# A scan kernel with its exponentials in another memory: `da` moved from PSUM to SBUF, banks and buffers shared out anew

## The chip, the cores and the metric

The kernel runs on one core of a Trainium2 chip. The metric is the time of one execution on the device, in microseconds. An engine is called by its short name in the profile: PE multiplies matrices, DVE is the vector engine, ACT the scalar engine, POOL the engine that the code calls `gpsimd`, SP the one whose queue issues the DMAs (`sync`). SBUF is the working memory; PSUM has eight banks of 128 x 512 fp32 values, into which PE writes.

## What is computed

The input is `x`, 8 images of 384 channels and 32 x 32 points, all in fp32. Layer 0 is a hybrid: a state-space recurrence in both directions along the 1024 points, plus a gated 3 x 3 convolution. Layer 1 is causal attention and a feed-forward network over the 1024 tokens. Cut to what matters here:

```python
# layer 0, for each direction
u = silu(conv1d(xn @ in_w)); z = xn @ in_w2
dt, Bm, Cm = split(u @ x_proj_w)
delta = softplus(dt @ dt_proj_w + dt_proj_b)
deltaA  = exp(delta[..., None] * A)                    # 16 states per channel
deltaBu = (delta * u)[..., None] * Bm[:, :, None, :]
h = dA * h + dBu                                       # along the 1024 points
y = (sum over states of h * C + u * D_param) * silu(z)
x = x + res_scale * ((fwd + bwd) @ out_w * scale_mod + sigmoid(conv2d(xn)) * xn)
# layer 1
t = t + attention(layernorm(t))                        # causal, one head
t = t + gelu(layernorm(t) @ kron(c_fc_1, c_fc_2).T) @ kron(c_proj_1, c_proj_2).T
```

## The kernel before, in words

**The recurrence.** A state of a channel takes a partition: 32 channels times 4 states fill the 128 partitions, and 512 points lie along the free axis. Each image (`b`) is worked off in four steps, `STEPS`: two directions times two halves of 512 points. A step has 12 units (3 groups of 128 channels `cc` times 4 groups of states `g`), so the kernel has 8 x 4 x 12 = 384 units. A unit (in `scan`) does the following:

- DMAs spread `delta` to four tiles `dl`, `delta * u` to one tile `du` of 128 x 2048 (a buffer of tag `hs`), and the rows of B and C to `br` and `cr`.
- POOL makes `hs = du * br` in one product of 128 x 2048.
- ACT makes four exponentials `da` of 128 x 512, at line 1054 in a buffer of the PSUM pool `ps_b` (5 banks).
- DVE runs four `tensor_tensor_scan` over `da` and `hs`. In a "split" unit the scan writes over `da`, and DVE then multiplies `da` by `cr` into `hs`. In the other units (`POOL_C`, 4 of 12; `POOL_END`, 5 of 12, in the last image) the scan writes into `hs` and POOL multiplies all of `hs` by `cr`.
- ACT copies the last column of a scan to `carry`, for the step that continues it.
- PE sums over the states by four matmuls `y <- hs, sel` into the PSUM bank `y`. D u comes in through one matmul with the diagonal matrix `ddiag`.

The last step of the last image is cut into two parts of 256 points.

**The rest.** `norm_in`, `raw_gate`, `conv_tokens`, `prepare`, `conv`, `local` and `gate` prepare the next image; `project` multiplies y by the output weights and adds the local branch and x; `attention` and `feed_forward` are layer 1, on halves of 512 tokens. All of it runs in between the units of the recurrence. PSUM is shared out as five banks for `da`, two for this side work (tag `w`, handed out by `bank`), one for `y`; in the last image's end `rota` lets the side work use `da` banks too. Transit tiles come in two pools, `tmp` (5) and `side` (4). The four large weights `win`, `wz`, `wout`, `wvs` are loaded once and stay. `prepare` sums u of two steps on POOL, so that D u enters once for both directions; `local` adds x on POOL.

**The order.** The program's instructions are recorded with a due time (`plan.due`, in units) and a margin (`plan.rush`). `Plan.order` then plays a model of the engines and issues, engine by engine, the most urgent instruction whose inputs and buffers would be there. It also places filler matmuls (`y <- zero, ident`) where PE would pause. So the constants at the head (`FIRST`, `OTHERS`, `LAYER1`, `SCAN` and others) are due times. Each engine executes its own queue in the order that this gave. In the profile nearly all instructions have line 460, the one in `issue` that calls them; they are told apart by their tiles.

Of the kernel before, what the change touches and what calls it, by code (L numbers as in the profile page):

```python
# [30 lines left out]
P = 128  # L31
# [4 lines left out]
TMP, SIDE = 5, 4  # L36
REPS = 4
RUSH = 3.54
START, LATER = -40.0, -8.0
# [3 lines left out]
FIRST = (1.62, 3.96, 10.3, 14.48, 18.18, 21.76)  # L43
SECOND = (22.86, 0.54)
OTHERS = (4.13, 9.04, 14.9, 17.86, 22.66, 25.08, 29.09, 34.25, 42.87, 49.8)
BURST = 8.07
PROJECT = 1.35
LAYER1 = (39.85, 51.29, 60.87, 72.21, 83.5)
LAYER1_6 = (43.34, 50.01, 57.44, 69.38, 72.99)
LAYER1_7 = (39.84, 42.87, 51.35, 57.52, 62.56, 71.14, 71.63, 74.06, 81.9)  # L50
HASTE = 26.32
FREE = ["w", "da", "w", "da"]
EXPS = -0.17
SCAN = (-1.49, -1.1, -0.44, -0.43, -0.36, 0.14, 0.08, 1.19, 0.79)
DU_AHEAD = 3.37
DL_AHEAD = 3.22
DLS = 5
DAS = 5
# [22 lines left out]
class Plan:  # L81
# [9 lines left out]
    LOOSE = ("w", "tmp", "side")  # L91
    HURRY = 8.29
    PATIENCE = 1.77
    TAIL = dict(tensor=0.21, vector=0.117, scalar=0.14, gpsimd=0.1, sync=0.1)
    RAW = 0.07
    NEXT = 0.01
    TURN = 0.1
# [203 lines left out]
    def order(self):  # L301
# [73 lines left out]
        while issued < total:  # L375
            best = None
            for e in engines:
                ts = [(at(op), op) for op in cand[e]]
                ts = [(t, op) for t, op in ts if t is not None]
                if not ts:  # L380
                    continue
                now = max(clock[e], min(t for t, _ in ts))
                if best is None or now < best[0]:
                    best = (now, e, ts)
# [3 lines left out]
            op = min((op for t, op in ts if t <= now), key=lambda op: op.rank)  # L388
# [14 lines left out]
            if e == "tensor" and self.nothing and now > clock[e]:  # L403

                y = [name for name in left_y if name in self.slot and users[name]]
                begun = bool(y) and left_y[y[0]] not in (0, all_y[y[0]])
                if begun or not y and max([last[n] for n in left_y if n in last], default=0.0) < clock[e]:
                    made = self._fill(max(array) + self.TURN * (form != (P, P)), now, begun)
                    started += made
                    if made:  # L410
                        array = [self.ran[-1][1]] * 4
                        form = P, P
                        now = max(now, array[0] + self.TURN * (op.form != form))
# [50 lines left out]
def conv_attn_kernel(  # L464
# [44 lines left out]
    ps_b = ctx.enter_context(tc.tile_pool(name="ps_b", bufs=1, space=bass.MemoryType.PSUM))  # L509
# [3 lines left out]
    rota = ["w"]  # L513

    def bank():
        rota.append(rota.pop(0))
        if rota[-1] == "w":
            return plan.tile(ps_w, [P, HB], "w", 8 - 1 - DAS)
        return plan.tile(ps_b, [P, HB], "da", DAS)
# [31 lines left out]
    win = load(in_wT[:, :C].rearrange("(cc p) e -> p cc e", p=P), [P, NC, C], "win")  # L551
# [25 lines left out]
    taps, flat = (plan.tile(l0, [P, HB], "side", SIDE)[: C // BC, :P] for _ in range(2))  # L577
# [21 lines left out]
    none = plan.tile(l0, [P, HB], "side", SIDE)[:, : NC * (WP + 1)]  # L599
# [13 lines left out]
    whose = plan.tile(l0, [P, HB], "side", SIDE)[:CG, :P]  # L613
# [23 lines left out]
    for cc in range(NC):  # L637
# [17 lines left out]
        plan.tile(l0, [P, HB], "side", SIDE)[: C // BC, : KW * KW * BC] for _ in range(2)  # L655
# [21 lines left out]
    wz = load(in_wT[:, C:].rearrange("(cc p) e -> p cc e", p=P), [P, NC, C], "wz")  # L677
    wout = load(out_wT.rearrange("(cc p) e -> p cc e", p=P), [P, NC, C], "wout")
    wvs = load(wv.rearrange("(cc p) e -> p cc e", p=P), [P, NC, C], "wvs")

    fc1s = weight([P, NF, P], "fc1s")
    for to in range(NG):
        for g in range(NG):
            plan.sync.dma_start(
                fc1s[to * NJ : (to + 1) * NJ, g::NG], fc1[g * NJ : (g + 1) * NJ]
            )
    fc1f = fc1s.rearrange("p f e -> p (f e)")
    plan.gpsimd.tensor_scalar_mul(fc1f, fc1f, 1.0 / NG)
# [20 lines left out]
    every = weight([P, NJ], "every")  # L709
    plan.vector.tensor_add(every, ident[:, :NJ], ident[:, NJ : 2 * NJ])  # L710
    for g in range(2, NG):
        plan.vector.tensor_add(every, every, ident[:, g * NJ : (g + 1) * NJ])
    emat = weight([P, NJ, NI], "emat")
    plan.vector.tensor_mul(
        emat,
        every.unsqueeze(2).to_broadcast([P, NJ, NI]),
        cp2.unsqueeze(1).to_broadcast([P, NJ, NI]),
    )
    emat = emat.rearrange("p j i -> p (j i)")
    plan.tile(ps_y, [P, HB], "y")  # L720
# [18 lines left out]
    def norm_in(b, h):  # L739
        xt = load_x(b, h)  # L740
        yield
# [36 lines left out]
    def raw_gate(b, h):  # L778

        xn, z = xn_t[b, h], plan.tile(dram, [P, NC, HB], "zr", 4)  # L780
# [51 lines left out]
    def local(b, h):  # L832

        cols = slice(h * HB, (h + 1) * HB)
# [4 lines left out]
        for cc in range(NC):  # L839
            xt = tmp()  # L840
            plan.sync.dma_start(xt, xv[b, :, cc, cols])
# [5 lines left out]
            plan.gpsimd.tensor_add(xt, xt, sg[:, cc])  # L847
            plan.sync.dma_start(lx[cc * P : (cc + 1) * P], xt)
# [55 lines left out]
    def prepare(b, steps):  # L904
# [45 lines left out]
        ud = ud_t[b, steps[0]] = plan.tile(dram, [C, HB], "ud", 4)  # L950
        for cc in range(NC):
            u = uc_t[b, steps[0]][:, cc]
            for si in steps[1:]:
                both = tmp()
                plan.gpsimd.tensor_add(both, u, uc_t[b, si][:, cc])
                u = both
            plan.sync.dma_start(ud[cc * P : (cc + 1) * P], u)
# [13 lines left out]
    def side():  # L971
        return plan.tile(l0, [P, HB], "side", SIDE)

    def scan(b, si, lo=0, hi=HB):
# [5 lines left out]
        ud = ud_t.get((b, si))  # L980
# [25 lines left out]
        for k in range(n_u):  # L1006
            cc, g = divmod(k, SG)
            t = t0 + f * k
            if g == 0:
# [19 lines left out]
                parts = []  # L1029
                if ud is not None:  # L1030
                    parts.append((ddiag[:, cc], ud[cc * P : (cc + 1) * P, lo:hi]))
# [6 lines left out]
                y = plan.tile(ps_y, [P, HB], "y")[:, :n]  # L1038
# [12 lines left out]
            for i in range(NQ):  # L1051
                j = cc * NQ + i
                plan.due, plan.rush = t + f * SCAN[1 + i], EXPS
                da = plan.tile(ps_b, [P, HB], "da", DAS)[:, :n]
# [7 lines left out]
                if split:  # L1062
                    if save:
                        plan.due, plan.rush = t + f * SCAN[5] * (i + 0.1), RUSH
                        plan.scalar.copy(carry[:, k, i : i + 1], da[:, 0:1] if d else da[:, n - 1 :])
                        plan.rush = 0.0
                    plan.due = t + f * (SCAN[5] * i + SCAN[6])
                    plan.vector.tensor_mul(hs[:, i], da, cr[g])
# [34 lines left out]
    def project(b, h, t1, lo=0, hi=HB):  # L1103

        yz = [yz_t[b, h, lo, cc] for cc in range(NC)]
        lx = []
        for cc in range(NC):
            lx.append(tmp()[:, : hi - lo])
            plan.sync.dma_start(lx[cc], lx_t[b, h][cc * P : (cc + 1) * P, lo:hi])
        yield  # L1110
        for i in range((hi - lo) // P):
# [7 lines left out]
            for cc in range(NC):  # L1119
                plan.tensor.matmul(  # L1120
                    po[:, cc * P : (cc + 1) * P], lx[cc][:, cols], ident,
                    start=False, stop=cc == NC - 1, is_transpose=True, skip_group_check=True,
                )
# [4 lines left out]
    def token_norm(t1, ti0, nt):  # L1128
# [9 lines left out]
        plan.gpsimd.tensor_scalar_mul(nrm[:, 1], mv[:, :, 0], -1.0)  # L1138
        plan.gpsimd.tensor_mul(nrm[:, 1], nrm[:, 1], nrm[:, 0])
# [12 lines left out]
    def attention(b, t1, t0, n, end=False):  # L1152
# [15 lines left out]
        for i in range(nt):  # L1168
            xt = normed(t1, tile0, nrm, i)
            pt = bank()  # L1170
            for cc in range(NC):
                plan.tensor.transpose(
                    pt[:, cc * P : (cc + 1) * P], xt[:, cc * P : (cc + 1) * P], ident
                )
            plan.scalar.copy(
# [18 lines left out]

        kp = turned(wks, "kp")
# [73 lines left out]
    def feed_forward(b, t1, t0, n, direct=False):  # L1269
# [4 lines left out]
        xr = plan.tile(l1, [P, NT, NJ], "xr")  # L1274
        for i in range(nt):
            xt = normed(t1, tile0, nrm, i).rearrange("p (j i) -> p j i", i=NI)
            plan.gpsimd.tensor_mul(xt, xt, c2.unsqueeze(1).to_broadcast([P, NJ, NI]))
            plan.vector.reduce_sum(xr[:, i], xt, axis=AX.X)
            yield
        px = bank()[:, :n]  # L1280
        for i in range(nt):
            for g in range(NG):
                plan.tensor.matmul(
                    px[g * NJ : (g + 1) * NJ, i * P : (i + 1) * P], xr[:, i], ident,
                    start=True, stop=True, skip_group_check=True,
# [6 lines left out]
        for f0 in range(0, NF, NF // 2):  # L1292
            gl = plan.tile(l1, [P, NF // 2, HB], "gl")[:, :, :n]
            for k in range(0, NF // 2, 2):
                ph = [bank()[:, :n], bank()[:, :n]]
                for i in range(2):
                    plan.tensor.matmul(ph[i], fc1s[:, f0 + k + i], xrT, start=True, stop=True)
# [10 lines left out]
            po = bank()[:, :n]  # L1308
            for k in range(NF // 2):
# [3 lines left out]
                    start=k < NG, stop=k >= NF // 2 - NG, skip_group_check=True,  # L1313
                )
            if f0 == 0:
                plan.scalar.copy(ob, po)
            else:
                plan.vector.tensor_add(ob, po, ob)
# [41 lines left out]
    for b in range(NB):  # L1360
# [21 lines left out]
        else:  # L1382
            first, rate = SECOND if b == 1 else (B - PER, 1.0)
            v = [first + rate * u for u in OTHERS]
# [12 lines left out]
        for si, (d, h) in enumerate(STEPS):  # L1397

            parts = ((0, HQ), (HQ, HB)) if last and si == 3 else ((0, HB),)
            for lo, hi in parts:  # L1400
                e = B + (si + hi / HB) * NU * SG
                scan(b, si, lo, hi)
                if si >= 2:
                    rota[:] = FREE if last and si == 3 and hi == HB else ["w"]
                    plan.rush = HASTE if last else 0.0
                    plan.spread(project(b, h, t1, lo, hi), e + 0.45, e + PROJECT)
                    plan.rush = 0.0
        rota[:] = ["w"]

        v = [B + u for u in (LAYER1 if b < NB - 2 else LAYER1_6 if not last else LAYER1_7)]  # L1410
# [7 lines left out]
        else:  # L1418
            for i in range(2):
                rota[:] = FREE if i else ["w"]  # L1420
                part = HB + i * HQ, HQ, i == 1
                plan.spread(attention(b, t1, *part), v[3 + i], v[5 + i])
                plan.spread(feed_forward(b, t1, *part), v[5 + i], v[7 + i])
# [74 lines left out]
```

## Time and profile before

| | us |
|---|---|
| time, median of 3 runs | 3051.7 (3050.02 to 3054.4) |
| the profiled execution: its own time | 3053.55 |
| the profiled execution: span | 3051.8 |
| busy: PE, DVE, ACT, POOL | 2698.0, 2700.1, 2175.5, 2686.7 |
| DMA: bytes moved, mean rate | 632.77 MB, 207 GB/s |
| granted PE clock | 0.969 |

A line of groups reads: line of code, engine, operation, tile written, an arrow, tiles read, shape; then how many, the busy time in us and the mean of one in ns; then the idle time of the engine ahead of them and what ended it. A line of the timeline begins with the start and the duration in us of a run of equal instructions. In the line of a stretch each engine's busy time stands with its number of instructions.

### The profile page before, as it was taken

How to read it: one execution, taken by the hardware profiler on the slowest of the kernel's cores; microseconds unless marked ns; L12 is line 12 of the kernel's file. 1: busy time of each engine (PE TensorE's matmuls, PEld its weight loads, DVE VectorE, ACT ScalarE, POOL GpSimd, SP SyncE). 2: the span in 40 equal slices, each digit the busy share in tenths (PEclk: the TensorE clock that was granted, in tenths of full speed). 3: DMA queues.
4: the chain of work that ended last, by engine and by line, in shares of the span. 5: the costliest groups of instructions: out<-in, count | busy, mean ns of one | idle time of the engine just before them, and what ended most of it. 6: DMA issues, size and time to landing. Idle time of an engine off the chain costs nothing. (4 is left out here: it accounts for less than half of the span.)

```text
span 3051.8 us, 39365 instructions
## 1 busy us (share of the span) xinstructions
PE 2698.0 (88%) x12021; PEld 1188.4 (39%) x12021; DVE 2700.1 (88%) x3514; ACT 2175.5 (71%) x3928; POOL 2686.7 (88%) x914
## 2 busy tenths in 40 slices
PE   8877897998999899988889898999989998988889
PEld 3322343343443434333343434434343433434445
DVE  3898938998899989998999979999899989999982
ACT  3765656778778786867768686787868687676774
POOL 2999868989898999989898999989998999999960
PEclk9988998999999999999999999999999999999999
DMA  7786776567766677666766667556775577533410
GB/s 249 242 275 215 230 263 221 183 225 251 240 202 200 221 259 229 201 205 223 244 194 204 225 217 251 198 193 224 258 231 186 201 242 254 168 131 121 149 54 17
DMA packets 345836, 632.77 MB, mean 207 GB/s; under 512 B 42544, under 2 KB 57208, under 8 KB 345624
## 3 DMA queue, kind: packets, MB, share of 16 engines
q1 hardware_dynamic: 345496, 630.14, 62.5%
q8 instruction: 95, 1.56, 0.2%
q14 instruction: 117, 0.96, 0.1%
q0 software_dynamic: 128, 0.11, 0.0%
HBM read 475.71 MB, written 154.38 MB: 206 GB/s over the span
## 5 line engine op out<-in xcount | busy, mean ns | idle before, releaser
L460 POOL TENSOR_TENSOR hs<-hs,br 128x2048 f32<-128x2048 f32 (+1 forms) x395 | 1739.0, 4418 | 167.8 <-PE y L460 85.2
L460 ACT ACTIVATE da<-dl,nega 128x512 f32<-128x512 f32 (+1 forms) x1584 | 1036.3, 676 | 402.5 <-DVE hs L460 386.4
L460 DVE TENSOR_TENSOR hs<-da,cr 128x512 f32<-128x512 f32 (+1 forms) x1036 | 656.8, 666 | 27.7 <-ACT carry L460 27.0
L460 DVE TENSOR_TENSOR_SCAN da<-da,carry,hs 128x512 f32<-128x512 f32 (+1 forms) x532 | 628.4, 1220 | 38.9 <-POOL hs L460 24.7
L460 DVE TENSOR_TENSOR_SCAN da<-da,hs 128x512 f32<-128x512 f32 x504 | 598.0, 1218 | 64.9 <-ACT da L460 48.4
L460 POOL TENSOR_TENSOR hs<-hs,cr 128x2048 f32<-128x2048 f32 (+1 forms) x137 | 600.1, 4380 | 54.4 <-DVE hs L460 31.4
L460 PE MATMUL y<-hs,sel 128*32 128x512 f32 (+1 forms) x3168 | 467.9, 616 | 97.3 <-POOL hs L460 81.1
L460 PE MATMUL y<-zero,ident 128*128 128x256 f32 x1470 | 387.9, 397 | 0.0
L460 DVE TENSOR_TENSOR_SCAN hs<-da,carry,hs 128x512 f32<-128x512 f32 (+1 forms) x284 | 324.1, 1192 | 13.0 <-ACT da L460 7.7
L460 PEld LDWEIGHTS y<-zero,ident 128*128 128x128 f32 x1470 | 271.2, 195 | 149.3 <-issue 119.1
L460 DVE TENSOR_TENSOR_SCAN hs<-da,hs 128x512 f32<-128x512 f32 x264 | 308.3, 1208 | 20.4 <-ACT da L460 19.4
L460 PEld LDWEIGHTS y<-hs,sel 128*32 128x32 f32 x3168 | 93.4, 111 | 337.7 <-issue 128.5
L458 ACT ACT_TABLE_LOAD x164 | 210.4, 1283 | 2.9
L460 PE MATMUL w<-q,fc1s 128*128 128x512 f32 (+1 forms) x396 | 198.2, 617 | 15.0 <-ACT gl L460 7.4
L460 PE MATMUL w<-v,p 128*128 128x384 f32 x562 | 200.8, 504 | 8.4 <-ACT p L460 4.7
L460 ACT COPY carry<-da 128x1 f32<-128x1 f32 x532 | 81.0, 163 | 170.8 <-DVE da L460 168.8
L460 PE MATMUL w<-rep,cit 96*32 96x512 f32 x1152 | 153.0, 606 | 9.4 <-DMA rep<-xq 7.3
L460 ACT COPY gl<-w 128x512 f32<-128x512 f32 (+2 forms) x254 | 137.5, 551 | 12.8 <-PE w L460 11.7
L460 PE MATMUL w<-wout,side 128*128 128x384 f32 x378 | 137.9, 503 | 7.9 <-ACT t L460 3.6
L460 PEld LDWEIGHTS w<-v,p 128*128 128x128 f32 x562 | 105.1, 194 | 90.9 <-ACT p L460 19.7
L460 PE MATMUL w<-xn,wz 128*128 128x512 f32 x288 | 132.8, 601 | 3.9 <-ACT tmp L460 3.4
L460 PE MATMUL w<-xn,win 128*128 128x512 f32 x288 | 130.7, 600 | 1.9 <-ACT tmp L460 0.9
(188 smaller groups left out, 3421.2 us busy)
## 6 DMA issues: line engine op xcount, KB each, us to landing
dl<-dd SPq DMA_DIRECT2D x372, 256.0 KB, 4.0
hs<-db SPq DMA_DIRECT2D x372, 256.0 KB, 4.5
rep<-up SPq DMA_DIRECT2D x180, 257.5 KB, 4.3
rep<-xq SPq DMA_DIRECT2D x192, 222.4 KB, 4.9
br<-bd SPq DMA_DIRECT2D x124, 256.0 KB, 4.6
cr<-bd SPq DMA_DIRECT2D x124, 256.0 KB, 4.3
tmp<-in_x_dram SPq DMA_DIRECT2D x96, 256.0 KB, 4.6
dd<-tmp SPq DMA_DIRECT2D x96, 256.0 KB, 3.4
```

What stands on the lines that cost most here:

```text
L458: self.nc.scalar.preload_act_table_set(table)
L460: op.call(*args, **{k: self._bind(v) for k, v in op.kw.items()})
```

## The change

- The exponentials `da` come from the SBUF pool `l0` (7 buffers) instead of the PSUM pool `ps_b`, which goes. The side work gets six banks `w`, `y` two; `rota` goes.
- `tmp` and `side` become one pool of 8. The four large weights take turns in two buffers `wt` and are loaded again for each image (`heavy`; `wvs` for each half).
- D u: `prepare` stores u of each step, and `scan` adds D u by `ddiag` in all four steps; POOL's sums go. x: `local` stores its gated part alone, and `project` loads x beside it and adds it by PE transposes; POOL's sum goes.
- `feed_forward`: the sum over 12 neighbours weighted by c2, made by POOL and DVE, becomes transposes and matmuls with `c2s`; `fc1s` is loaded once instead of four times and used by rows; the second half's sum is taken in PSUM by a matmul with `ident`.
- `token_norm`: two small POOL operations become one of DVE. In `scan` the multiply stands ahead of the carry copy.
- The planner looks no further than `SIGHT` ahead and puts off a change of ACT's table by `YIELD`; due times are new, some by image.

```diff
-TMP, SIDE = 5, 4
+TMP = 8
+YS = 2
+WTS = 2
...
-DAS = 5
+DAS = 7
...
+    SIGHT = 48.0
+    YIELD = 6
...
-        rota.append(rota.pop(0))
-        if rota[-1] == "w":
-            return plan.tile(ps_w, [P, HB], "w", 8 - 1 - DAS)
-        return plan.tile(ps_b, [P, HB], "da", DAS)
+        return plan.tile(ps_w, [P, HB], "w", 8 - YS)
...
+    def heavy(nm, key):
+
+        if (nm, key) not in big:
+            src = dict(win=in_wT[:, :C], wz=in_wT[:, C:], wout=out_wT, wvs=wv)[nm]
+            t = big[nm, key] = plan.tile(const, [P, NC, C], "wt", WTS)
+            plan.sync.dma_start(t, src.rearrange("(cc p) e -> p cc e", p=P))
+        return big[nm, key]
...
-    fc1s = weight([P, NF, P], "fc1s")
-    for to in range(NG):
-        for g in range(NG):
-            plan.sync.dma_start(
-                fc1s[to * NJ : (to + 1) * NJ, g::NG], fc1[g * NJ : (g + 1) * NJ]
-            )
-    fc1f = fc1s.rearrange("p f e -> p (f e)")
-    plan.gpsimd.tensor_scalar_mul(fc1f, fc1f, 1.0 / NG)
+    fc1s = load(fc1, [P, NF // NG, P], "fc1s")
...
-            xt = tmp()
-            plan.sync.dma_start(xt, xv[b, :, cc, cols])
             xn = reps()[:, : HR * WP]
...
-            plan.gpsimd.tensor_add(xt, xt, sg[:, cc])
-            plan.sync.dma_start(lx[cc * P : (cc + 1) * P], xt)
+            plan.sync.dma_start(lx[cc * P : (cc + 1) * P], sg[:, cc])
...
-        ud = ud_t[b, steps[0]] = plan.tile(dram, [C, HB], "ud", 4)
-        for cc in range(NC):
-            u = uc_t[b, steps[0]][:, cc]
-            for si in steps[1:]:
-                both = tmp()
-                plan.gpsimd.tensor_add(both, u, uc_t[b, si][:, cc])
-                u = both
-            plan.sync.dma_start(ud[cc * P : (cc + 1) * P], u)
+        for si in steps:
+            ud = ud_t[b, si] = plan.tile(dram, [C, HB], "ud", 8)
+            for cc in range(NC):
+                plan.sync.dma_start(ud[cc * P : (cc + 1) * P], uc_t[b, si][:, cc])
...
-                da = plan.tile(ps_b, [P, HB], "da", DAS)[:, :n]
+                da = plan.tile(l0, [P, HB], "da", DAS)[:, :n]
...
                 if split:
+                    plan.due = t + f * (SCAN[5] * i + SCAN[6])
+                    plan.vector.tensor_mul(hs[:, i], da, cr[g])
                     if save:
...
-                    plan.due = t + f * (SCAN[5] * i + SCAN[6])
-                    plan.vector.tensor_mul(hs[:, i], da, cr[g])
...
+            lx.append((tmp()[:, : hi - lo], reps()[:, : hi - lo]))
+            plan.sync.dma_start(lx[cc][0], lx_t[b, h][cc * P : (cc + 1) * P, lo:hi])
+            plan.sync.dma_start(lx[cc][1], xv[b, :, cc, h * HB + lo : h * HB + hi])
...
-        plan.gpsimd.tensor_scalar_mul(nrm[:, 1], mv[:, :, 0], -1.0)
-        plan.gpsimd.tensor_mul(nrm[:, 1], nrm[:, 1], nrm[:, 0])
+        plan.vector.scalar_tensor_tensor(
+            nrm[:, 1], mv[:, :, 0], -1.0, nrm[:, 0], ALU.mult, ALU.mult
+        )
...
-            xt = normed(t1, tile0, nrm, i).rearrange("p (j i) -> p j i", i=NI)
-            plan.gpsimd.tensor_mul(xt, xt, c2.unsqueeze(1).to_broadcast([P, NJ, NI]))
-            plan.vector.reduce_sum(xr[:, i], xt, axis=AX.X)
+            xt = normed(t1, tile0, nrm, i)
+            pt = bank()
...
-        for i in range(nt):
+        for cc in range(NC):
             for g in range(NG):
                 plan.tensor.matmul(
-                    px[g * NJ : (g + 1) * NJ, i * P : (i + 1) * P], xr[:, i], ident,
-                    start=True, stop=True, skip_group_check=True,
+                    px[g * NJ : (g + 1) * NJ], c2s[:, cc], xT[:, cc],
+                    start=cc == 0, stop=cc == NC - 1, skip_group_check=True,
                 )
...
-            if f0 == 0:
-                plan.scalar.copy(ob, po)
-            else:
-                plan.vector.tensor_add(ob, po, ob)
+            plan.scalar.copy(ob, po)
```

## The prediction

> **What bounds the kernel now.** I read the page first: the busy shares, then the costliest groups.
>
> ```profile
> PE 2698.0 (88%) x12021; PEld 1188.4 (39%) x12021; DVE 2700.1 (88%) x3514; ACT 2175.5 (71%) x3928; POOL 2686.7 (88%) x914
> ...
> L460 POOL TENSOR_TENSOR hs<-hs,br 128x2048 f32<-128x2048 f32 (+1 forms) x395 | 1739.0, 4418 | 167.8 <-PE y L460 85.2
> ...
> L460 DVE TENSOR_TENSOR hs<-da,cr 128x512 f32<-128x512 f32 (+1 forms) x1036 | 656.8, 666 | 27.7 <-ACT carry L460 27.0
> L460 DVE TENSOR_TENSOR_SCAN da<-da,carry,hs 128x512 f32<-128x512 f32 (+1 forms) x532 | 628.4, 1220 | 38.9 <-POOL hs L460 24.7
> L460 DVE TENSOR_TENSOR_SCAN da<-da,hs 128x512 f32<-128x512 f32 x504 | 598.0, 1218 | 64.9 <-ACT da L460 48.4
> L460 POOL TENSOR_TENSOR hs<-hs,cr 128x2048 f32<-128x2048 f32 (+1 forms) x137 | 600.1, 4380 | 54.4 <-DVE hs L460 31.4
> ```
>
> DVE and POOL are both 88% busy over the whole span. The busy time by stretch shows that the rest is mostly the two ends:
>
> ```profile
> 61.00:2900.00 2839.00, 2507.62 (x11147) 1087.71 (x11148) 2603.67 (x3273) 2064.36 (x3701) 2629.02 (x863) 0.97 0.65 216
> ```
>
> Between 61 and 2900 us (columns PE, PEld, DVE, ACT, POOL) DVE is at 92% and POOL at 93%. PE's figure contains 388 us of `y<-zero,ident` filler matmuls. So two engines set the pace together, and they can because they work side by side. The timeline of a steady stretch shows it:
>
> ```profile
> 700.47 18.21 POOL L460 TENSOR_TENSOR hs<-hs,br 128x2048 f32<-128x2048 f32 x4
> ...
> 705.97 2.34 DVE L460 TENSOR_TENSOR_SCAN da<-da,hs 128x512 f32<-128x512 f32 x2
> 708.22 1.27 DVE L460 TENSOR_TENSOR hs<-da,cr 128x512 f32<-128x512 f32 x2
> 709.40 3.44 DVE L460 TENSOR_TENSOR_SCAN hs<-da,hs 128x512 f32<-128x512 f32 x3
> ```
>
> Four POOL products run without a gap (4.55 each) while DVE's scans keep 1.2 us and its multiplies 0.63. In every one of these DVE instructions one tensor, `da`, is in PSUM and the other in SBUF. The change moves `da` to SBUF, so I looked for DVE instructions that already have two SBUF tensors. There are few. The first unit's product is the one that meets POOL (the instructions of tile hs on DVE between 57 and 67 us, then the timeline):
>
> ```profile
> L460 DVE TENSOR_TENSOR hs<-hs,br x4: 675/686/4987, 57.2 to 61.6; 128x512 f32<-128x512 f32 x4
> ...
> 60.42 1.27 DVE L460 TENSOR_TENSOR hs<-hs,br 128x512 f32<-128x512 f32 x2
> 61.60 4.99 DVE L460 TENSOR_TENSOR hs<-hs,br 128x512 f32<-128x512 f32 x1
> ...
> 61.20 4.84 POOL L460 TENSOR_TENSOR hs<-hs,br 128x2048 f32<-128x2048 f32 x1 [47.49 <-DMA zr<-tmp]
> ```
>
> Three of the four take 0.68. The one that starts while a POOL product runs takes 4.99: it ends at 66.59, 0.55 after POOL's end at 66.04. POOL's own 4.84 is 0.32 over its usual 4.52: its start fell into the DVE multiply before. Each waited for the other's whole instruction. This pair of rows decides the forecast.
>
> **The change part by part.**
>
> *Exponentials in SBUF.* All 1584 scans (first tensor `da`, second `hs`) and 1036 `cr` multiplies get two SBUF inputs; POOL's 626 products read SBUF as before. The row shows the exclusion for a multiply; no row has a scan with two SBUF inputs. The Trainium skill ("SBUF — State Buffer", Who interferes with whom) states it for any DVE instruction with two SBUF inputs against a GpSimd instruction that reads SBUF: the pair of ports is locked for a whole instruction and the other blocks fully. By the row alone only the multiplies would collide (second rival, 4250); by the page the scans too. A scan reads two streams as a multiply does, so I follow the page. Then DVE's recurrence and POOL's products no longer lie beside each other: they add.
>
> DVE's part, by distances between starts, since rows overlap slightly: scans without carry 1.125 (705.97 to 708.22 is two), with carry 1.185 (2.37 for two in the steady stretch at 201 us), multiplies 0.59. 768 x 1.125 = 864; 720 x 1.185 = 853; 96 half ones x 0.645 = 62; 980 x 0.59 = 578; 56 half ones x 0.32 = 18. Sum 2375.
> POOL's part at 4.47 from start to start (200.27 to 204.73): 498 x 4.47 = 2226; 34 halves x 2.32 = 79; 93 `uc<-uc,tmp` x 1.22 = 113; 48 `uc<-uc,rep` x 1.14 = 55. Sum 2473.
> Both: 4848. Handing over costs nothing visible (0.55 after POOL, against 0.59 between free multiplies), so no surcharge.
>
> Around it: 59 us before the first scan and 88 us after the last `hs` multiply (2963.8) to the end, neither shortened nor lengthened: 4848 + 147 = 4995. DVE's remaining work in the middle (norm statistics, maxima of scores, `xn`, `side`, `t`; some 270 us of rows, 230 by distances) has at most one large SBUF input and may run under a POOL product, if it stands at the head of DVE's queue then. None to all of it is covered; I take half: +115. Stretches in which neither works: 0 to 250 (today's DVE idle time in the middle is 235, and POOL works in most of it); I take 60. Sum 5170.
>
> Does the access itself get cheaper? The skill ("Perfetto Trace Analysis", Optimizing Scalar/DVE Operations) gives DVE about 60 ns of overhead on SBUF and 125 on PSUM, and ScalarE 93 and 51. By the page 2620 DVE instructions would save 170 us and 1584 exponentials cost 67 us more. The trace doesn't show it: a multiply with two SBUF inputs takes 0.675 to 0.692, with one in PSUM 0.680, 0.59 apart both. An ACT copy from PSUM to SBUF takes 0.580, an activation from PSUM to PSUM 0.586. I take nothing for either; with the page's figure the sum would be 5000.
>
> *Work taken off POOL.* `local` 48 x 1.274 = 61, `prepare` 45 x 1.274 = 56 (56.2 in the rows), c2 products 57, small norm operations 15, fc1 scaling 4: 193 us, already absent from the 2473. Off DVE: 64 reductions `xr` 34 and 16 sums `ob` 11, less 34 tiny `nrm` products; about 40.
>
> *Work put on PE, ACT and DMA.* Transposes of x in `project`, as `w<-ident,tmp` now: +33 us PE. Some 45 more `ddiag` matmuls (55.1 for 51 now): +50. Transposes of the normed tokens +33, `c2s` matmuls for the `xr` ones about +10, `ob` by `ident` +18. That is +145 on an engine with 2310 us without fillers. ACT: 64 copies of 0.476 and 15 of 0.58, about +40 on 2175. SP issues 45 more stores and 48 more loads of `ud` and 37 more weight loads, less 15 of fc1: 115 on 2446, some 0.5 us each (the `fc1s` and `ud` issues in the timeline), so 58 us of SP's time, and about 45 MB on 633. The x loads leave `local` for `project`, where each call takes three `rep` buffers of four ahead of whatever conv load stands behind on SP. All of this is hidden under 5000 us of DVE and POOL. If that cover were absent, PE would stand at (2310 + 145) / 3052 = 80% and ACT at 73%, still short of a bound; what a late `rep` load could stop is a `dl` or `hs` load, prefetched over three units ahead. Taken as nothing; bounds -20 and +60.
>
> *PSUM 6 + 2 banks, seven `da`, dues, looser order.* They remove waits such as `POOL hs <- PE y` (85), `DVE da <- ACT da` (58) and, with the multiply now ahead of the carry copy, `DVE hs <- ACT carry` (28). In a sum of two engines that exclude each other such waits are filled by the other one: nothing. The bound is already in the 0 to 250.
>
> **The rivals.**
> 1. *The long row was a single accident.* For: it is one instance. Against: both rows fit to 0.1 us, and the waits that the trace shows end before either row begins. Then POOL drops to about 2500 and DVE alone is the bound: 2604 - 40 = 2564 in the middle, plus about 140 of idle time, plus 213 for the ends: 2917, say 2920, faster. The point of decision: the change can give back some 135 us at best, over 626 POOL products that is 0.2 us each. The row shows 4.3.
> 2. *Scans don't collide, multiplies do.* A product then hides fully under the four scans of an unsplit unit (4.6 us, a quarter of DVE's time) and by 0.6 to 0.8 elsewhere: 5170 - 620 - 300 = 4250.
> 3. *It is worse than the sum*: the order written for side-by-side engines makes the other queues late too, so that neither works for 10 to 15% of the time: 5600 to 5900.
> That `da` might not move is excluded: the tile's pool is `l0` instead of the PSUM pool.
>
> **How the numbers follow.** Sum of both engines 86%, rival 1 5%, rival 2 5%, rival 3 4%. The likeliest case alone spans 4900 (all side work covered, no idle) to 5500 (none covered, 250 idle, some disorder). About a tenth of it lies outside; with the others some 2 in 10, so this is the range. The profiled execution took 3053.55 for a span of 3051.8, the median is 3051.7: no correction is due. A measurement can tell about 0.2% (6 us) from no change; faster comes from rival 1 alone: 5%, same 1%, slower 94%.
>
> **What would show it.** Right: the rows of `hs<-da,cr` and of the scans far above 0.67 and 1.2 in the mean, with single ones near 5 us; their sum with POOL's 2473 close to the span, so that DVE's busy share reads near 100% though it does less; POOL's products above 4.5; PE and ACT shares nearly halved. Wrong: scans at 1.2 beside POOL's products (rival 2, or 1 if multiplies too), or a large idle share on DVE and POOL alike (rival 3).

## The result and the profile after

The changed kernel takes 5134.16 us in the median of four runs (5130.64 to 5137.01), against 3051.42 before, also over four: the ratio is 1.682, with a 95% interval of 1.679 to 1.685. The forecast was 5170, range 4900 to 5500.

The page of the changed kernel, its busy shares and the groups that answer to those shown of before:

```profile
PE 3357.0 (65%) x12146; PEld 1321.2 (26%) x12146; DVE 4891.4 (95%) x3469; ACT 2252.7 (44%) x4015; POOL 2890.2 (56%) x688
...
L489 POOL TENSOR_TENSOR hs<-hs,br 128x2048 f32<-128x2048 f32 (+1 forms) x395 | 1946.5, 4938 | 850.9 <-PE y L489 509.5
L489 DVE TENSOR_TENSOR hs<-da,cr 128x512 f32<-128x512 f32 (+1 forms) x1036 | 1723.5, 1694 | 0.8
...
L489 POOL TENSOR_TENSOR hs<-hs,cr 128x2048 f32<-128x2048 f32 (+1 forms) x137 | 685.4, 5003 | 1111.8 <-ACT carry L489 532.3
L489 DVE TENSOR_TENSOR_SCAN da<-da,carry,hs 128x512 f32<-128x512 f32 (+1 forms) x532 | 1112.8, 2126 | 22.7 <-POOL hs L489 17.8
L489 DVE TENSOR_TENSOR_SCAN da<-da,hs 128x512 f32<-128x512 f32 x504 | 1123.4, 2260 | 6.0 <-ACT da L489 6.0
...
L489 DVE TENSOR_TENSOR_SCAN hs<-da,hs 128x512 f32<-128x512 f32 x264 | 368.1, 1440 | 11.9 <-ACT da L489 11.9
```

The same number of multiplies takes 1.694 us in the mean instead of 0.666, the scans of split units 2.1 to 2.3 instead of 1.22. The 548 scans of the other units grow only to 1.37 to 1.44, from 1.19 to 1.21: while they run, POOL's queue mostly stands at the `cr` product that needs their results (1112 us idle ahead of `hs<-hs,cr`). DVE looks 95% busy, but a row that is blocked counts as busy. The time is in the rows themselves, not in the idle time ahead of them: no semaphore wait explains it. The spread tells more than the mean (DVE's instructions on tile da; durations as least, median, greatest; one line of before, then three of the changed kernel):

```profile
L460 DVE TENSOR_TENSOR hs<-da,cr x1036: 393/680/699, 73.5 to 2963.4; 128x512 f32<-128x512 f32 x164, 128x256 f32<-128x256 f32 x9
...
L489 DVE TENSOR_TENSOR hs<-da,cr x1036: 392/680/5046, 69.2 to 5028.6; 128x512 f32<-128x512 f32 x164, 128x256 f32<-128x256 f32 x9
L489 DVE TENSOR_TENSOR_SCAN da<-da,carry,hs x532: 718/1271/5615, 217.5 to 5027.7; 128x512 f32<-128x512 f32 x159, 128x256 f32<-128x256 f32 x19
L489 DVE TENSOR_TENSOR_SCAN da<-da,hs x504: 1165/1212/5541, 59.2 to 4860.3; 128x512 f32<-128x512 f32 x168
```

The medians are within 8 ns of those of before (680, 1273, 1220). A free instruction is as fast as ever; some wait for a whole POOL product. The timeline shows how it goes, the rows of POOL and DVE put in order of time:

```profile
2513.78 5.41 POOL L489 TENSOR_TENSOR hs<-hs,cr 128x2048 f32<-128x2048 f32 x1 [3.06 <-DVE sm L489]
2514.91 4.83 DVE L489 TENSOR_TENSOR hs<-da,cr 128x512 f32<-128x512 f32 x1
2519.14 4.96 POOL L489 TENSOR_TENSOR hs<-hs,br 128x2048 f32<-128x2048 f32 x1
2519.66 5.53 DVE L489 TENSOR_TENSOR_SCAN da<-da,carry,hs 128x512 f32<-128x512 f32 x1
2524.07 5.41 POOL L489 TENSOR_TENSOR hs<-hs,br 128x2048 f32<-128x2048 f32 x1
2525.11 5.45 DVE L489 TENSOR_TENSOR_SCAN da<-da,carry,hs 128x512 f32<-128x512 f32 x1
```

They take turns. The product that starts at 2513.78 ends at 2519.19; the multiply beside it ends at 2519.74, 0.55 later. The next product has started by then and waits in turn for that multiply: its row is 0.4 longer than a free one, and it ends 4.36 after the multiply. In 16 us DVE gets three instructions done.

### The profile page after: what moved, and what is told of

Same layout as the page of the kernel before. It is cut to its first block, busy times and chain, and to the rows that moved or that the text cites. A ratio compares the mean times of both kernels' runs of the same rounds, so it can differ in the third digit from the quotient of the medians.

```text
span 5130.8 us, 40014 instructions
## 1 busy us (share of the span) xinstructions
PE 3357.0 (65%) x12146; PEld 1321.2 (26%) x12146; DVE 4891.4 (95%) x3469; ACT 2252.7 (44%) x4015; POOL 2890.2 (56%) x688
## 5 line engine op out<-in xcount | busy, mean ns | idle before, releaser
L489 POOL TENSOR_TENSOR hs<-hs,br 128x2048 f32<-128x2048 f32 (+1 forms) x395 | 1946.5, 4938 | 850.9 <-PE y L489 509.5
L489 DVE TENSOR_TENSOR hs<-da,cr 128x512 f32<-128x512 f32 (+1 forms) x1036 | 1723.5, 1694 | 0.8
L489 PE MATMUL y<-hs,sel 128*32 128x512 f32 (+1 forms) x3168 | 935.2, 729 | 980.8 <-DVE hs L489 898.7
L489 DVE TENSOR_TENSOR_SCAN da<-da,carry,hs 128x512 f32<-128x512 f32 (+1 forms) x532 | 1112.8, 2126 | 22.7 <-POOL hs L489 17.8
L489 DVE TENSOR_TENSOR_SCAN da<-da,hs 128x512 f32<-128x512 f32 x504 | 1123.4, 2260 | 6.0 <-ACT da L489 6.0
L489 PE MATMUL w<-xn,wt 128*128 128x512 f32 x576 | 290.0, 646 | 27.9 <-DVE xn L489 27.4
L489 POOL TENSOR_TENSOR uc<-uc,tmp 128x512 f32<-128x512 f32 x93 | 175.1, 1912 | 99.9 <-ACT tmp L489 95.9
L489 ACT COPY gl<-w 128x384 f32<-128x384 f32 (+2 forms) x318 | 158.5, 530 | 51.7 <-PE w L489 51.1
L489 PEld LDWEIGHTS w<-xn,wt 128*128 128x128 f32 x576 | 113.1, 207 | 185.2 <-issue 132.5
L489 PE MATMUL w<-wt,tmp 128*128 128x384 f32 x384 | 148.8, 523 | 17.7 <-DVE tmp L489 17.7
```

Of the source, the lines that this page charges most:

```text
L489: op.call(*args, **{k: self._bind(v) for k, v in op.kw.items()})
```

## The experiments

**e1 to e4: which instructions collide.** Four kernels on one base: the changed kernel with 4 + 3 + 1 PSUM banks and a line in `project` (`plan.joint`) by which a bank is taken together with the row of `t1` that it is copied to. They differ in where the scan and the multiply find their first tensor. The base, e1:

```diff
-YS = 2
+YS = 1
-DAS = 7
+DAS = 4
+    ps_b = ctx.enter_context(tc.tile_pool(name="ps_b", bufs=1, space=bass.MemoryType.PSUM))
-        return plan.tile(ps_w, [P, HB], "w", 8 - YS)
+        return plan.tile(ps_w, [P, HB], "w", 8 - YS - DAS)
-                da = plan.tile(l0, [P, HB], "da", DAS)[:, :n]
+                da = plan.tile(ps_b, [P, HB], "da", DAS)[:, :n]
+            plan.joint = [t1[:, h * NT + lo // P + i]]
```

> The changed kernel with the exponentials back in PSUM: 4 banks for da, 3 for side work, 1 for y; everything else of the change stays (weights in turns, sums on PE, new due times). Theory A (DVE instructions with two SBUF inputs and POOL's products exclude each other): DVE and POOL run side by side again, POOL with 190 us less work than before and DVE with 40 us less: 2920 to 3050, scans at 1.2 us, multiplies at 0.67, POOL's products at 4.5. Theory B (the loss comes from the other edits: the order, the due times, the reloads): stays above 4500.

e2, against e1 (`ps_b` still keeps its four banks from the side work):

```diff
-                da = plan.tile(ps_b, [P, HB], "da", DAS)[:, :n]
+                da = plan.tile(l0, [P, HB], "da", 7)[:, :n]
```

> As e1, with one line more than the place of da differing in nothing: da in 7 SBUF buffers, still 3 banks for side work and 1 for y. Theory A: within 2% of the changed kernel, 5100 to 5200, so that the place of da alone makes the loss. Theory B2 (it needs the six side banks and the two y banks too): clearly apart from 5134.

e3, against e1 (not shown: the carry copy then reads `hs`, and stands ahead of the multiply again):

```diff
-                o, a, r = hs[:, i], da, da if split else hs[:, i]
+                o, a, r = hs[:, i], da, hs[:, i]
-                    plan.vector.tensor_mul(hs[:, i], da, cr[g])
+                    plan.vector.tensor_mul(hs[:, i], hs[:, i], cr[g])
```

> As e1 (da in PSUM), but the scan of a split unit writes into hs, and the multiply works on hs in place: only the 1036 multiplies have two SBUF inputs, the scans have one. Theory A: POOL's products hide under the scans of unsplit units and under about one scan elsewhere, 4000 to 4400; multiplies near 2 us in the mean with single ones near 5, scans at 1.2. Theory C (an exclusion only for scans): as e1, about 3000.

e4, against e1 (not shown: the carry copy then reads `dr`):

```diff
-                da = plan.tile(ps_b, [P, HB], "da", DAS)[:, :n]
+                da = plan.tile(l0, [P, HB], "da", 7)[:, :n]
-                o, a, r = hs[:, i], da, da if split else hs[:, i]
+                dr = plan.tile(ps_b, [P, HB], "dr", DAS)[:, :n] if split else None
+                o, a, r = hs[:, i], da, dr if split else hs[:, i]
-                    plan.vector.tensor_mul(hs[:, i], da, cr[g])
+                    plan.vector.tensor_mul(hs[:, i], dr, cr[g])
```

> As e1, but da in SBUF and the scan of a split unit writes into a PSUM bank, from which the multiply reads: only the 1584 scans have two SBUF inputs, the multiplies have one. Theory A: a product of POOL hides only under part of a multiply, 626 x 0.3 us less than both together: 4850 to 5050; scans near 2.2 us in the mean, single ones near 5.6, multiplies at 0.67. Theory D (an exclusion only for multiplies, the second rival of the prediction): as e1, about 3000.

| two SBUF inputs in | us |
|---|---|
| e1: none | 3198.15 (ratio to before 1.047, 1.045 to 1.049) |
| e3: the multiplies | 4472.59 |
| e4: the scans | 4857.48 |
| e2: both | 5204.04 |

e2, e3, e4 and, below, e6 were timed once each; the steps that are read from them are hundreds of microseconds.

The page of e1, and DVE's groups by form, first of e1, then e3, e4 and e2:

```profile
PE 2811.3 (88%) x12382; PEld 1238.5 (39%) x12382; DVE 2728.9 (85%) x3469; ACT 2239.0 (70%) x4025; POOL 2504.1 (78%) x688
...
L489 DVE TENSOR_TENSOR hs<-da,cr 128x512 f32<-128x512 f32 x980 | 633.1, 676 | 1.8
L489 DVE TENSOR_TENSOR_SCAN da<-da,hs 128x512 f32<-128x512 f32 x504 | 593.2, 1212 | 78.6 <-ACT da L489 66.4 <-POOL hs L489 9.8 <-issue 2.5
```

```profile
L489 DVE TENSOR_TENSOR hs<-hs,cr 128x512 f32<-128x512 f32 x980 | 1927.3, 1995 | 30.2 <-ACT carry L489 29.2
L489 DVE TENSOR_TENSOR_SCAN hs<-da,hs 128x512 f32<-128x512 f32 x768 | 892.4, 1201 | 63.8 <-ACT da L489 58.7 <-issue 3.3 <-POOL hs L489 0.9
```

```profile
L489 DVE TENSOR_TENSOR_SCAN dr<-da,hs 128x512 f32<-128x512 f32 x504 | 1303.4, 2620 | 33.4 <-ACT da L489 19.5 <-POOL hs L489 6.9 <-issue 3.6
L489 DVE TENSOR_TENSOR hs<-dr,cr 128x512 f32<-128x512 f32 x980 | 628.7, 672 | 0.7
```

```profile
L489 DVE TENSOR_TENSOR hs<-da,cr 128x512 f32<-128x512 f32 x980 | 1522.6, 1583 | 1.2
```

Of the scans and multiplies, e3 and e4 stretch exactly those with two SBUF inputs and leave the other kind at 0.67 or 1.20 (without carry). There is no exception: the longest of e3's 1584 scans takes 1.29, and the longest of e4's 1036 multiplies 0.69. So scans collide as multiplies do, which no row of before could say. The two effects (+1274 and +1659) don't add up to the joint one (+2006); both fit in the same POOL products. e2 is 1.4% above the changed kernel (4 us above its range), so the place of `da` makes the loss with or without the six side banks. e1 missed its range on the upper side, and e3 did because it stands on e1: its step over e1, 1274, is within the 1015 to 1415 that its range left over an e1 of 2985, the middle of e1's range. Theories B, B2, C and D fall.

**e5 and e6: adding up, and reading against writing.** e5 gives all `cr` multiplies of the changed kernel to DVE. e6 does so too, and leaves out the product with `br`, so that POOL writes `hs` without reading:

```diff
-POOL_C = (2, 5, 8, 10)
-POOL_END = (1, 3, 6, 8, 10)
+POOL_C = ()
+POOL_END = ()
-                plan.gpsimd.tensor_mul(hs, du, br[g].unsqueeze(1).to_broadcast([P, NQ, n]))
+                plan.gpsimd.memset(hs, 0.5)
```

(the last pair of lines in e6 alone)

> The changed kernel with POOL_C and POOL_END empty: DVE makes all cr multiplies, POOL only the br products. Theory A (the two engines add up): POOL loses 127 x 4.47 + 10 x 2.3 = 591 us, DVE gains 508 x 0.59 + 40 x 0.32 = 313 us, so 278 us faster than 5134: 4800 to 4900, although DVE, the busier engine, gets more to do. Theory E (DVE is slow for a reason of its own and POOL lies beside it): 313 us slower, about 5450.

> As e5, but POOL's products hs = du * br are replaced by a memset of hs, which writes SBUF and reads nothing: this leaves the product out of the computation. If POOL's reading collides with the second input of DVE: scans at 1.2 and multiplies at 0.67 again, DVE alone is the bound, 2375 + 313 + 230 of DVE and 147 for the ends, with idle time 3050 to 3250. If POOL's writing collides as well: the memsets' own time comes on top, and single DVE rows are as long as a memset.

e5 took 4887.56, 247 us less than the changed kernel, although the busier engine got 313 us more to do (estimated from the distances between starts): the two engines' times add up, and a multiply is cheaper on DVE. e6 took 3262.47, 12 above its range. Its groups on DVE and POOL:

```profile
L489 DVE TENSOR_TENSOR hs<-da,cr 128x512 f32<-128x512 f32 x1488 | 1024.8, 721 | 0.7
L489 DVE TENSOR_TENSOR_SCAN da<-da,hs 128x512 f32<-128x512 f32 x768 | 930.3, 1246 | 10.2 <-ACT da L489 8.3 <-POOL hs L489 1.8
...
L489 POOL MEMSET hs<- 128x2048 f32 x371 | 665.4, 1806 | 1898.4 <-PE y L489 1515.6 <-DMA hs<-db 221.3 <-PE w L489 56.0
L489 POOL TENSOR_TENSOR uc<-uc,tmp 128x512 f32<-128x512 f32 x93 | 171.5, 1876 | 134.3 <-ACT tmp L489 81.2 <-DMA hs<-db 35.9 <-ACT carry L489 12.2
```

Beside 665 us of memsets the scans and multiplies are free: counted row by row in the trace, the 953 that overlap a memset take no longer, in sum, than the medians of their kinds. The whole excess over the medians, 128 us, lies in the 177 rows that overlap one of POOL's 141 small products, which still read: 93 of these take 1.88 instead of 1.28, 48 take 1.83 instead of 1.18. I had left their 168 us out of the expectation; with them it is 2375 + 313 + 230 + 147 + 168 = 3233. So POOL's reading collides with DVE's second input, and its writing doesn't. The Trainium skill says the same of an instruction that only writes ("SBUF — State Buffer", Who interferes with whom), and this trace agrees. Nor is ACT's writing the cause: it writes `da` to SBUF in e6 too.

**e7 to e11: is there a faster version?** All but e8 start from the kernel before, keep `da` in its five PSUM banks and take over parts of the change. e7: D u by `ddiag` in all steps, x in `project`, c2 by PE. e9: the first two. e10: the multiply ahead of the carry copy. e11: e9 and e10. e8 starts from e1 and gives `token_norm` its POOL operations back. The edits are hunks of the diff above.

> The kernel before, with its banks (da in PSUM, 5 banks), pools and due times, and with three parts of the change alone: D u in all four steps by ddiag, x added by transposes in project, the c2 sums by PE. POOL loses 174 us and DVE 34. If the bound is DVE with POOL close behind: 2604 - 34 = 2570 in the middle, 150 to 235 of idle time, 213 for the ends, 2930 to 3020, faster than before by 1 to 4%. If the order, written for the old costs, eats it: 3040 to 3100.

> As e1 (da in PSUM, 4 + 3 + 1 banks), but token_norm keeps its two small POOL operations of before. In e1 the tiny DVE product nrm<-mv,nrm has two SBUF inputs and takes 2.1 us in the mean, where its operands would take 0.1: 30 x 2 us of waiting for POOL. Theory A: up to 60 us faster than e1, 3130 to 3180. If DVE's waiting there was covered: as e1, 3198.

> The kernel before with two parts of the change alone: D u in all steps and x in project, both by PE. POOL loses 117 us; PE gets 83 us more, but no further PSUM banks are asked for. Against e7 the c2 sums stay on POOL and DVE. If e7 is slow because the c2 sums need more turns of two side banks (transpose, copy, matmul): 3000 to 3050, not slower than before. If e7 is slow because of the ddiag matmuls ahead of the one y bank and of the x loads in rep: about as e7, 3080 to 3140.

> The kernel before, with the multiply recorded and due ahead of the carry copy, as in the change. DVE's multiplies waited 28 us for ACT's carry copies. If that waiting lay on DVE's path: up to 28 us faster, 3020 to 3050. If other waits take its place: 3051, the same.

> e9 and e10 together, as the version that could beat both kernels: 2970 to 3040 if both help, otherwise about as the worse of the two.

| | us | ratio to before |
|---|---|---|
| e7 | 3137.26 | 1.028 (1.026 to 1.030) |
| e8 | 3161.73 | 1.036 (1.034 to 1.038) |
| e9 | 3103.04 | 1.017 (1.015 to 1.018) |
| e10 | 3085.30 | 1.011 (1.009 to 1.012) |
| e11 | 3125.59 | 1.024 (1.023 to 1.026) |

None beats the kernel before; e7 and e10 came out above all that was expected of them, e11 23 us above the slower of its two parts. e7 did take the work off, as its page shows, and two of its waits show a part of what ate it:

```profile
PE 2777.6 (89%) x12218; PEld 1216.7 (39%) x12218; DVE 2675.0 (85%) x3452; ACT 2220.9 (71%) x4003; POOL 2520.4 (80%) x757
...
POOL hs L460 <- PE y L460: 185.4, 59, 11.7
...
DVE da L460 <- ACT da L460: 80.1, 44, 6.7
```

POOL has 166 us less to do and DVE 25, yet DVE's idle time grew from 352 to 463. POOL now waits 185 us for PE to give back a buffer of `hs` (85 before), and DVE 80 for exponentials (58); the rest of DVE's 111 us is spread over many waits. e9 shows that the c2 sums are only part of it, e10 that even a swap of two neighbours costs 1%: DVE's 28 us of waiting for carry copies go, others come (50 us for POOL products, 37 before; 72 for exponentials, 58 before). What the runs do not settle is whether new due times would turn these edits into a gain. The order of before was left as it is in e7, e9, e10 and e11; fitting it again wasn't tried.

e8 settles one thing. In e1 the tiny product of `token_norm`, which the change moved to DVE, has two SBUF inputs (the instructions of tile nrm on DVE):

```profile
L489 DVE SCALAR_TENSOR_TENSOR nrm<-mv,nrm x34: 144/1744/4308, 398.0 to 3165.2; 128x4 f32<-128x4 f32 x30, 128x2 f32<-128x2 f32 x4
```

Four columns take up to 4.3 us, so being small doesn't help. 23 of the 34 are stretched, and each of these ends 0.02 us after a POOL product. With this work back on POOL, 36 of the some 60 us are regained.

## Why the prediction was right, point by point

- *The step that decided*, one 4.99 us row for a two-SBUF multiply and its 4.84 us partner, was no accident. Rival 1 fell with the changed kernel, rival 2 with e4: the scans collide. Rival 3 fell too: DVE and POOL stand idle together for 78 us. That the scans would collide no row of before had shown; e4 does.
- *The sum.* Laying the rows of DVE's scans and multiplies and of POOL over each other, the changed kernel has 59 us before the first scan, 4752 in which at least one of the two works, 140 of DVE's other work that no POOL row covers, 78 in which neither works, and 102 after the last multiply: 5131. Forecast were 59, 4848, 115, 60 and 88. The joint term was 96 too large, and the three after it 25, 18 and 14 too small. The first two of these were guesses (half of 230, and 60 out of 0 to 250), so part of the closeness of 5170 to 5134 is luck; the range did not need it. "So no surcharge" was right, but handing over even saves time. Counted in the trace, 265 scans end 1.08 after the POOL product that blocked them (free ones 1.125 to 1.185 apart), 256 multiplies 0.55 (0.59), and 451 products 4.32 after the DVE instruction that blocked them (4.47). By these medians that is some 90 to 105 us, an estimate which covers the 96. The prediction's "626 products" should read 673 (`hs` and `uc` products together); its sum of 2473 has all of them.
- *DVE's access to SBUF at no gain* was right: the medians stayed, and the 170 us that the prediction worked out from the skill's page did not come. *ACT's at no cost* was mis-sized, as the exponentials by form show, e1 with PSUM first, then the changed kernel with SBUF:

```profile
L489 ACT ACTIVATE da<-dl,nega 128x512 f32<-128x512 f32 x1488 | 999.3, 690 | 351.7 <-DVE hs L489 315.5 <-DMA dl<-dd 16.5 <-DVE sm L489 8.0
```

```profile
L489 ACT ACTIVATE da<-dl,nega 128x512 f32<-128x512 f32 x1488 | 1024.5, 718 | 1318.7 <-DVE hs L489 1116.6 <-issue 126.6 <-DVE sm L489 52.3
```

  Writing to SBUF costs 28 ns each, 44 us over 1584; the figures of the Trainium skill ("Perfetto Trace Analysis", Optimizing Scalar/DVE Operations) gave 42 ns. e2 has 718 as well, with e1's side banks. ACT had the room. My comparison (a copy from PSUM to SBUF against an activation within PSUM) put two kinds of instruction side by side.
- *The 34 `nrm` products* were written off as tiny. In e1 they cost some 60 us of DVE's rows; in the changed kernel they took 33.5.
- *Work moved to PE, ACT and SP at nothing* held under 5000 us of DVE and POOL. Without that cover it doesn't: rival 1 priced the rest of the change at 2920, and e1, with da in PSUM on fewer banks, takes 3198; how much of that is due to the banks isn't shown.
- *The signs.* Long single rows, DVE near 100% and POOL's products above 4.5 came as named. The sign "their sum with POOL's 2473 close to the span" was put wrongly: stretched rows contain the waiting for POOL, so DVE's scans and multiplies alone fill 4622 us; it is their free time, 2375, that adds to 2473. ACT's share fell to 44%, and PE's, which got slower (below), only to 65%; "nearly halved" fits neither well.

## What to carry to other kernels

Before a tensor moves from PSUM to SBUF, count the SBUF inputs of every DVE instruction that reads it: here an instruction with two of them did not run beside a POOL product, which reads SBUF, and two engines at 88% each became one chain of 168% of the old time. A memset on POOL did no harm. One odd row (a mean far above its median, in a group of four) can carry such a forecast; look for the instruction that already is what the change makes of the others. And removing work from an engine that sets the pace is no gain by itself where the order is written for the old costs: e7 and e9 took work off POOL and lost 1.7 to 2.8%.

## What the runs showed of the hardware that was not expected

The granted PE clock fell from 0.969 to 0.786 in the changed kernel and came back with its speed: 0.942 in e1, 0.968 in e6, between them 0.831 in e3. PE's rows grew with it, for the same matmuls: `y<-hs,sel` takes 0.729 in the mean against 0.616. PE is busy 3357 us against 2698; some 110 of that is work that the change puts on PE, since e1 has 2811 at a clock of 0.942. In the slow kernels PE also waits longer for DVE's `hs` between its groups of four matmuls (460 us in e3, 175 in e6), but what lowers the clock isn't shown by these runs. Here PE waits for DVE anyway (898.7 us for `hs`), so this cost was covered; it is the main reason why PE's share didn't halve.
